# Gaussian elimination split between VectorE and GpSimd: the last eight rows of 128 small systems

## The chip, the cores and the metric

The kernel runs on one core of one Trainium2 chip, as one program of some 90,000 instructions. The metric is the time of one execution on the device in microseconds (us). Before the change the median of three runs is 5004.54 us (5003.34 to 5005.09).

## The reference

Twelve residual blocks act on x, 128 batch entries of 32 tokens with 128 channels. The change touches L0's attention, a kernel attention that solves a linear system for each batch entry and head. Its core, for each of the 128 x 16 pairs of entry and head (8 channels a head):

```python
landmarks = K[:, :, landmark_idx, :]                  # 64 indices into the 32 tokens
Phi_Q = jnp.exp(-C_Q / temperature)                   # C_Q, C_K: squared distances to the landmarks
Phi_K = jnp.exp(-C_K / temperature)
W_kernel = jnp.exp(-W_sq / temperature) + REG * jnp.eye(NUM_LANDMARKS)
Y = jnp.linalg.solve(W_kernel, jnp.einsum('bhnk,bhnd->bhkd', Phi_K, V))
out_unnorm = jnp.einsum('bhnk,bhkd->bhnd', Phi_Q, Y)  # divided by the same with V of ones
```

Since the 64 landmarks are drawn from 32 tokens, the kernel solves a system of 32 rows with 9 right-hand sides (8 value columns and one of ones), with the square roots of each token's count as a diagonal scaling.

The output projection of this is added to x. Before it comes a cross-attention of each entry to 257 context rows with 16 heads; after it comes a feed-forward layer with 8 experts of which each token takes two.

## The kernel before

**Stages.** `L0_xattn` (lines 372 to 476) loops over the 128 batch entries, n = 0 to 127, in eight groups g of 16. For each entry it computes scores on TensorE (S, line 544), takes their maxima on VectorE (L546, L547), exponentials on ScalarE (L548, L558), transposes (L566, L569), multiplies with the context (L583, L584); for each tile of four entries it computes queries (L527) and the output (L597). The last VectorE instruction of an entry is L555 (it writes TL). Evacuations of queries (L528) and of OT (L585) are ScalarE's. Then `L0_ffn` (lines 857 to 911) routes tokens to experts, and the rest of L1 to L3 follows.

**Side work.** L0's attention for a group runs beside the cross-attention of later groups, in generators that yield after each piece:

- `L0_attn_kernels(g)` (613 to 685), in the queue `kq`: phi_k and phi_q. Its masks (M, L249), weights (PW, L671 and L672) and blocked values (Vb, L690) run on GpSimd, except in the last group, where they run on VectorE.
- `L0_attn_solve(g)` (693 to 739), in `sq`: the elimination. Once a group's kernels are written, its solve is appended.
- `L0_attn_out(g)` (741 to 773), in `oq`: four output tiles (Yb, ko, O, kot, kw), appended when the solve ends.

`side_steps` (318) is called after every entry with `side_steps(3, 8)`: three pieces of `kq`, then pieces of `sq` until their yielded costs, in us, sum to 8, then one of `oq`. The yielded number is the planner's own guess of VectorE time. In `L0_ffn` the budgets are 3.0, 4.0 and 6.5. A scheduler then sets the final order of each engine's instructions; TensorE's order in the cross-attention is also fixed by manual dependences (`follow`, `queue`).

**The solve.** A has 128 partitions (16 entries x 8 pairs of heads), and on each the two systems side by side: `A[p, i, h, j]`, 32 rows i, 2 heads h, 41 columns j (32 and 9 right-hand sides). For pivot k: the pivot is clamped and inverted (L712, L713), the scaled row is written to `row` (L716, two buffers), and the rows below are updated in blocks of eight (`RB`): a product into `elt` (L722), then a subtraction in A (L724). In the end ScalarE copies the scaled row back into A (L726). Line 729 and 731 are the back substitution. All of it but the copy is VectorE's. The block of rows 24 to 31 has m x 2 x n = 8 x 2 x 17 = 272 elements a partition for pivots 0 to 23.

Other places that the change touches: `dispatch` makes one-hot tiles SL (L845, three buffers) for 16 small matmuls in each of four calls; `L0_ffn_back` gathers expert outputs into G (six buffers) by GpSimd's indirect DMA, 16 in each of four calls, and adds them to x (L1026).

Of the kernel before, what the change touches and what calls it, by code (L numbers as in the profile page):

```python
# [9 lines left out]
FP = mybir.dt.float32  # L10
# [3 lines left out]
ALU = mybir.AluOpType  # L14
# [4 lines left out]
B, T, C = 128, 32, 128  # L19
NG = 8  # L20
# [148 lines left out]
class Kern:  # L169
# [523 lines left out]
    def L0_attn_solve(self, g):  # L693


        nc, sv = self.nc, self.sv
        HC, R, RB = 2, HD + 1, 8
        N = T + R
        A = sv.tile([128, T, HC, N], FP, tag="A", bufs=2)
        bs = slice(16 * g, 16 * g + 16)  # L700
        wv = self.wd.rearrange("(b n) (g h q) -> g h b n q", n=T, g=8, h=HC)
        zv = self.zd.rearrange("b n (g h e) -> g h b n e", g=8, h=HC)
        for hg in range(8):
            r = slice(16 * hg, 16 * hg + 16)
            for h in range(HC):
                nc.sync.dma_start(A[r, :, h, 0:T], wv[hg, h, bs])
            for h in range(HC):
                (nc.scalar if g == NG - 1 else nc.sync).dma_start(A[r, :, h, T:N], zv[hg, h, bs])
        yield 1.0
        for k in range(T):  # L710
            p = sv.tile([128, HC], FP, tag="p", bufs=2)
            nc.vector.tensor_scalar(p, A[:, k, :, k], 1e-6, None, ALU.max)  # L712
            nc.vector.reciprocal(p, p)  # L713
            n = N - 1 - k
            row = sv.tile([128, HC, N], FP, tag="row", bufs=2)
            nc.vector.tensor_tensor(row[:, :, k + 1:N], A[:, k, :, k + 1:N], p.unsqueeze(2).to_broadcast([128, HC, n]), ALU.mult)  # L716
            yield 0.3 + 0.00107 * HC * n
            for i0 in range((k + 1) // RB * RB, T, RB):
                i0, i1 = max(i0, k + 1), i0 + RB
                m, n = i1 - i0, N - i0  # L720
                t = sv.tile([128, RB * HC * N], FP, tag="t", name="elt")[:, :m * HC * n].rearrange("p (i h j) -> p i h j", i=m, h=HC)
                nc.vector.tensor_tensor(t, A[:, k, :, i0:i1].rearrange("p h i -> p i h").unsqueeze(3).to_broadcast([128, m, HC, n]),  # L722
                                        row[:, :, i0:N].unsqueeze(1).to_broadcast([128, m, HC, n]), ALU.mult)
                nc.vector.tensor_tensor(A[:, i0:i1, :, i0:N], A[:, i0:i1, :, i0:N], t, ALU.subtract)  # L724
                yield 0.12 + 0.00214 * m * HC * n
            nc.scalar.copy(A[:, k, :, k + 1:N], row[:, :, k + 1:N])  # L726
        for k in range(T - 1, 0, -1):
            t = sv.tile([128, RB * HC * N], FP, tag="t", name="elt")[:, :k * HC * R].rearrange("p (i h j) -> p i h j", i=k, h=HC)
            nc.vector.tensor_tensor(t, A[:, 0:k, :, k:k + 1].to_broadcast([128, k, HC, R]),
                                    A[:, k, :, T:N].unsqueeze(1).to_broadcast([128, k, HC, R]), ALU.mult)  # L730
            nc.vector.tensor_tensor(A[:, 0:k, :, T:N], A[:, 0:k, :, T:N], t, ALU.subtract)
            yield 0.12 + 0.00214 * k * HC * R
        Yt = sv.tile([128, RB * HC * N], FP, tag="t", name="Yt")[:, :T * HC * R].rearrange("p (i h j) -> p i h j", i=T, h=HC)
        nc.scalar.copy(Yt, A[:, :, :, T:N])
        yv = self.yd.rearrange("b n (g f) -> g b n f", g=8)
        for hg in range(8):
            nc.sync.dma_start(yv[hg, bs], Yt[16 * hg:16 * hg + 16].rearrange("p i h j -> p i (h j)"))
        self.oq.append(chain([1] * (3 if g < NG - 2 else 0), self.L0_attn_out(g)))
        yield 0.1
# [37 lines left out]
    def dispatch(self, pool, psum, tag, I8, n, k, E, NB):  # L777

        nc = self.nc
# [25 lines left out]
        t = pool.tile([128, E, n], FP, tag="dt")  # L805
# [35 lines left out]
        yield 1  # L841
        ps = psum.tile([128, NB], FP, tag=tag, name="pinv")
        for i in range(n * k):
            SL = pool.tile([128, 128], FP, tag="dSL", bufs=3)
            nc.vector.tensor_scalar(SL, self.j128, qf[:, i, 0:1], None, ALU.is_equal)  # L845
            nc.tensor.matmul(ps, lhsT=SL, rhs=BK[:, i, :], start=i == 0, stop=i == n * k - 1)
            if i % 4 == 3 and i < n * k - 1:
                yield 1
# [170 lines left out]
    def L0_ffn_back(self, m, c, slot, rows, inv, E2, fs):  # L1019
        nc = self.nc  # L1020
        for i in range(8):
            x = self.X[c[i // 4]][:, i % 4, :]
            for j in range(2):
                G = fs.tile([128, 128], FP, tag="G", bufs=6)
                self.gather(G, self.ysd[m], slot[:, i, j:j + 1])
                nc.vector.scalar_tensor_tensor(x, G, E2[:, i, j:j + 1], x, ALU.mult, ALU.add)  # L1026

# [59 lines left out]
    def depool(self, dp, dps, tag):  # L1087
# [32 lines left out]
        for g in range(NG):  # L1120
# [17 lines left out]
            nc.scalar.activation(m, m, AF.Exp, scale=-DT)  # L1138
            G = dp.tile([128, 4, 4, T], FP, tag="G")
            nc.vector.scalar_tensor_tensor(G.rearrange("p i b t -> p (i b t)"), PB, self.pm, m, ALU.is_ge, ALU.mult)  # L1140
            nc.gpsimd.tensor_tensor(G, G, bm, ALU.mult)
            ps = dps.tile([128, 4, 128], FP, tag=tag, name="pdp")
            for i in range(4):
                nc.tensor.matmul(ps[:, i, :], lhsT=G[:, i, :, :], rhs=Uc[:, i, :], start=True, stop=True)
            Dg = dp.tile([128, 4, 128], FP, tag="Dg")
# [789 lines left out]
```

## Time and profile before

| | |
|---|---|
| runs before, median | 5004.54 us (5003.34 to 5005.09) |
| the profiled execution's own time | 5007.62 us |
| its span, first to last instruction | 5005.9 us |
| mean granted TensorE clock | 0.889 |
| busy: TensorE, VectorE, ScalarE, GpSimd | 85%, 68%, 47%, 26% |
| L722 and L724, VectorE | 608 each, 290.0 and 291.2 us |
| L729 and L731, VectorE | 248 each, 126.6 and 126.5 us |
| L0's cross-attention | until about 2108 us |
| solves, first pivot row to end of the copy of Y | from 449.8 us to 2423.1 us |

Engines are PE (TensorE's matmul), PEld (its weight load), DVE (VectorE), ACT (ScalarE), POOL (GpSimd), SP (SyncE). A row of the groups reads: line, engine, operation, tile written <- tiles read, shape, xcount | busy us, mean ns of one | idle time of the engine just before, and what ended it. A row of the windows gives each engine's busy time in a stretch. The timeline gives start in us, length, engine, line, operation.

### The profile page before, as it was taken

What the parts mean: (1) busy time and instruction counts of PE and PEld (TensorE: products, weight loads), DVE (VectorE), ACT (ScalarE), POOL (GpSimd) and SP (SyncE); (2) the same over time, 40 slices, a digit from 0 to 9 for tenths busy, and PEclk for the clock granted to TensorE, in tenths of its full rate; (3) what the DMA queues carried; (4) which work ended last, traced back from release to release, by engine and by line L of the source; (5) the groups of instructions that cost most, each with busy time, mean ns of one, the idle gap of its engine ahead of it and who ended that gap; (6) DMA issues with size and microseconds to landing.
All of it is one profiled execution on the core that took longest, in us unless ns stands there. A gap on an engine that the chain in (4) does not pass through costs nothing. (4 is left out here: it accounts for less than half of the span.)

```text
span 5005.9 us, 90275 instructions
## 1 busy us (share of the span) xinstructions
PE 4248.2 (85%) x33802; PEld 3111.7 (62%) x33802; DVE 3387.4 (68%) x10311; ACT 2347.2 (47%) x6637; POOL 1295.6 (26%) x1309
## 2 busy tenths in 40 slices
PE   7999999999898999875377798898898886879788
PEld 5777676767676776665365565666566653546455
DVE  5336758494948576777655478888898775777444
ACT  4555445454444444432233354545554554763333
POOL 1020211111110202035143513332332332322443
PEclk8999899999999998967677898999999987989677
DMA  4223131314141222255132410111011101000100
GB/s 139 61 60 57 39 66 42 66 39 72 38 72 35 56 53 56 49 121 144 37 107 86 138 35 23 31 29 28 27 29 32 37 20 46 1 1 16 32 14 10
DMA packets 388968, 255.95 MB, mean 51 GB/s; under 512 B 184545, under 2 KB 356961, under 8 KB 388017
## 3 DMA queue, kind: packets, MB, share of 16 engines
q1 hardware_dynamic: 361842, 191.22, 16.1%
q0 software_dynamic: 18240, 58.66, 4.0%
q8 instruction: 266, 4.36, 0.4%
q10 hardware_dynamic: 8448, 0.30, 0.2%
q14 instruction: 172, 1.41, 0.1%
HBM read 211.02 MB, written 39.08 MB: 50 GB/s over the span
## 5 line engine op out<-in xcount | busy, mean ns | idle before, releaser
L218 POOL TENSOR_TENSOR rs<-ve,w_const 128x4 f32<-128x4 f32 (+1 forms) x192 | 189.9, 990 | 1552.1 <-DVE ve L216 1278.4
L544 PE MATMUL S<-cT,q 128*128 128x257 f32 x2048 | 545.5, 407 | 18.5 <-ACT E L548 17.8
L544 PEld LDWEIGHTS S<-cT,q 128*128 128x128 f32 x2048 | 391.0, 201 | 145.7 <-issue 54.6
L546 DVE TENSOR_REDUCE nm<-S 128x1 f32<-128x257 f32 x512 | 214.8, 420 | 335.9 <-PE S L544 334.6
L1389 PE MATMUL S<-cT,QM 128*128 128x289 f32 x1024 | 326.4, 435 | 78.5 <-ACT E L1391 70.5
L548 ACT ACTIVATE E<-S,nm 128x257 f32<-128x257 f32 x512 | 242.3, 474 | 299.8 <-DVE nm L547 298.8
L1391 ACT ACTIVATE E<-S,nm 128x289 f32<-128x289 f32 x512 | 253.4, 499 | 194.8 <-DVE nm L1390 190.9
L722 DVE TENSOR_TENSOR elt<-A,row 128x400 f32<-128x400 f32 (+22 forms) x608 | 290.0, 477 | 6.4
L724 DVE TENSOR_TENSOR A<-A,elt 128x400 f32<-128x400 f32 (+22 forms) x608 | 291.2, 479 | 4.2
L527 PE MATMUL pq<-xT,WQK 128*128 128x128 f32 x2048 | 268.0, 290 | 14.1 <-ACT q L528 14.1
L1389 PEld LDWEIGHTS S<-cT,QM 128*128 128x128 f32 x1024 | 177.5, 198 | 161.8 <-ACT E L1391 72.3
L583 PE MATMUL po<-TA,cN 128*128 128x512 f32 x512 | 271.1, 612 | 4.7 <-DVE xn L224 3.9
L527 PEld LDWEIGHTS pq<-xT,WQK 128*128 128x128 f32 x2048 | 252.5, 200 | 24.7 <-ACT q L528 17.6
L584 PE MATMUL po<-TB,cN 128*128 128x512 f32 x512 | 265.5, 600 | 0.0
L558 ACT ACTIVATE E<-E,sm 128x256 f32<-128x256 f32 x512 | 220.2, 498 | 79.8 <-DVE sm L554 74.9
L241 POOL TENSOR_TENSOR QM<-QT,w_const 128x512 f32<-128x512 f32 x128 | 142.6, 1119 | 434.0 <-PE S L1389 410.7
L1390 DVE TENSOR_REDUCE nm<-S 128x1 f32<-128x289 f32 x512 | 219.8, 449 | 31.1 <-PE S L1389 28.3
L1400 PE MATMUL pt<-w_const,E 128*96 128x128 f32 (+1 forms) x1536 | 234.9, 290 | 0.0
L597 PE MATMUL pout<-WVO,OT 128*128 128x128 f32 x2048 | 234.2, 276 | 0.3 <-ACT OT L585 0.3
L597 PEld LDWEIGHTS pout<-WVO,OT 128*128 128x128 f32 x2048 | 231.7, 192 | 0.9 <-ACT OT L585 0.5
L1400 PEld LDWEIGHTS pt<-w_const,E 128*96 128x96 f32 (+1 forms) x1536 | 181.5, 145 | 61.6 <-issue 37.3
L1721 ACT ACTIVATE E<-S,nm 128x128 f32<-128x128 f32 x512 | 179.9, 397 | 64.6 <-DVE nm L1718 64.6
(526 smaller groups left out, 10357.3 us busy)
## 6 DMA issues: line engine op xcount, KB each, us to landing
cT<-ctxT SPq DMA_DIRECT2D x128, 257.0 KB
cN<-ctx SPq DMA_DIRECT2D x128, 256.0 KB
cT<-ctxT SPq DMA_DIRECT2D x32, 514.0 KB
phik<-PW SPq DMA_DIRECT2D x32, 256.0 KB
phiq<-P SPq DMA_DIRECT2D x32, 256.0 KB
A<-phik SPq DMA_DIRECT2D x128, 64.0 KB
PQ<-phiq SPq DMA_DIRECT2D x32, 256.0 KB
cN<-ctx SPq DMA_DIRECT2D x32, 194.0 KB
```

The source lines that it names most:

```text
L527: self.follow(st, nc.tensor.matmul(ps[:, k, :, :], lhsT=WQK[:, 4 * j + k, cb * 128:(cb + 1) * 128], rhs=t["x"], start=True, stop=True))
L544: self.follow(st, nc.tensor.matmul(S, lhsT=t["QP"][j][:, cb, b, :, :], rhs=t["cT"][b][:, cb, :], start=cb == 0, stop=cb == 1))
L548: nc.scalar.activation(E[:, j, 0:LK], S, AF.Exp, bias=m, accum_out=sm[:, j:j + 1])
L558: nc.scalar.activation(E[:, j, 0:256], E[:, j, 0:256], AF.Copy, scale=sm[:, j:j + 1])
L583: self.follow(st, nc.tensor.matmul(po, lhsT=cN[:, 0, c], rhs=TA, start=True, stop=False), nc.tensor.matmul(po, lhsT=cN[:, 1, c], rhs=TB, s ...
L584: nc.tensor.matmul(po, lhsT=cN[:, 1, c], rhs=TB, start=False, stop=True))
L597: self.follow(st, nc.tensor.matmul(po[:, 0, :], lhsT=OT[:, cb, h, :, :], rhs=WVO[:, cb, h, :], start=h == 0 and cb == 0, stop=False))
L722: nc.vector.tensor_tensor(t, A[:, k, :, i0:i1].rearrange("p h i -> p i h").unsqueeze(3).to_broadcast([128, m, HC, n]), row[:, :, i0:N].uns ...
L724: nc.vector.tensor_tensor(A[:, i0:i1, :, i0:N], A[:, i0:i1, :, i0:N], t, ALU.subtract)
L1389: self.follow(st, nc.tensor.matmul(S, lhsT=t["QM"][:, 0, 4 * j:4 * j + 4, :], rhs=t["cT"][:, b, :], start=True, stop=True))
L1391: nc.scalar.activation(E[:, j, :], S, AF.Exp, bias=nm[:, j:j + 1], accum_out=sm[:, j, b:b + 1])
L1400: self.follow(st, nc.tensor.transpose(pt[0:n, j * 128:(j + 1) * 128], E[:, j, k0:k1], self.ident))
```

## The change

In the solves of groups 0 to 6, the product and the subtraction of the last block (rows 24 to 31, while it is whole, that is for pivots 0 to 23) are GpSimd's, with a buffer of their own (`eltp`), and count 0.01 in the planner's sum. The scaled row has three buffers. To make room, SL has two buffers and G three. The last group's solve stays on VectorE.

```diff
-            row = sv.tile([128, HC, N], FP, tag="row", bufs=2)
+            row = sv.tile([128, HC, N], FP, tag="row", bufs=3)
...
-                nc.vector.tensor_tensor(t, A[:, k, :, i0:i1].rearrange("p h i -> p i h").unsqueeze(3).to_broadcast([128, m, HC, n]),
-                                        row[:, :, i0:N].unsqueeze(1).to_broadcast([128, m, HC, n]), ALU.mult)
-                nc.vector.tensor_tensor(A[:, i0:i1, :, i0:N], A[:, i0:i1, :, i0:N], t, ALU.subtract)
-                yield 0.12 + 0.00214 * m * HC * n
+                eng = nc.vector
+                if g < NG - 1 and i0 == T - RB:
+                    eng = nc.gpsimd
+                    t = sv.tile([128, RB * HC * (RB + R)], FP, tag="tp", name="eltp").rearrange("p (i h j) -> p i h j", i=m, h=HC)
+                eng.tensor_tensor(t, A[:, k, :, i0:i1].rearrange("p h i -> p i h").unsqueeze(3).to_broadcast([128, m, HC, n]),
+                                  row[:, :, i0:N].unsqueeze(1).to_broadcast([128, m, HC, n]), ALU.mult)
+                eng.tensor_tensor(A[:, i0:i1, :, i0:N], A[:, i0:i1, :, i0:N], t, ALU.subtract)
+                yield 0.12 + 0.00214 * m * HC * n if eng is nc.vector else 0.01
...
-            SL = pool.tile([128, 128], FP, tag="dSL", bufs=3)
+            SL = pool.tile([128, 128], FP, tag="dSL", bufs=2)
...
-                G = fs.tile([128, 128], FP, tag="G", bufs=6)
+                G = fs.tile([128, 128], FP, tag="G", bufs=3)
```

## The prediction

> **What bounds the kernel now.** The page gives busy shares first.
>
> ```profile
> PE 4248.2 (85%) x33802; PEld 3111.7 (62%) x33802; DVE 3387.4 (68%) x10311; ACT 2347.2 (47%) x6637; POOL 1295.6 (26%) x1309
> ```
>
> TensorE leads, but these shares average over stages. The groups say what the change touches:
>
> ```profile
> L722 DVE TENSOR_TENSOR elt<-A,row 128x400 f32<-128x400 f32 (+22 forms) x608 | 290.0, 477 | 6.4
> L724 DVE TENSOR_TENSOR A<-A,elt 128x400 f32<-128x400 f32 (+22 forms) x608 | 291.2, 479 | 4.2
> ```
>
> VectorE never waits before these 581 us of elimination. By shape, the part that moves (columns as on the page):
>
> ```profile
> L724 DVE TENSOR_TENSOR A<-A,elt 128x272 f32<-128x272 f32 x192 | 84.0, 437 | 0.2
> L722 DVE TENSOR_TENSOR elt<-A,row 128x272 f32<-128x272 f32 x192 | 83.2, 433 | 1.5
> ```
>
> The stage decides. I cut one group of 16 batch entries (1507.8 to 1776.5 us, 268.7 us) at the ends of the L555 row, which closes each entry; call the stretches A, B, C and so on. Columns: length, then busy PE, PEld, DVE, ACT, POOL, granted clock, DMA share, GB/s.
>
> ```profile
> 1507.80:1540.30 32.50, 27.08 (x187) 21.74 (x186) 24.89 (x79) 12.23 (x33) 1.27 (x1) 0.84 0.09 26
> 1540.30:1550.80 10.50, 10.26 (x64) 8.00 (x63) 8.82 (x33) 6.02 (x19) 0.00 (x0) 1.00 0.18 52
> 1550.80:1568.80 18.00, 16.50 (x83) 11.63 (x82) 17.84 (x61) 5.99 (x20) 2.38 (x4) 1.00 0.12 32
> 1568.80:1576.90 8.10, 8.07 (x53) 6.48 (x52) 7.97 (x31) 6.61 (x21) 0.00 (x0) 1.00 0.23 65
> 1576.90:1593.20 16.30, 14.54 (x76) 11.02 (x76) 15.99 (x60) 9.62 (x28) 0.00 (x0) 1.00 0.12 34
> 1593.20:1601.50 8.30, 7.96 (x47) 6.03 (x46) 8.16 (x34) 5.79 (x20) 0.00 (x0) 1.00 0.23 64
> 1601.50:1626.10 24.60, 19.64 (x168) 14.24 (x169) 21.81 (x88) 10.97 (x34) 7.68 (x9) 1.00 0.08 24
> 1626.10:1645.70 19.60, 17.44 (x228) 11.91 (x218) 18.89 (x42) 9.84 (x27) 6.67 (x5) 0.87 0.16 46
> 1645.70:1669.30 23.60, 23.44 (x246) 18.95 (x242) 22.20 (x58) 11.65 (x27) 5.13 (x4) 0.82 0.14 48
> 1669.30:1684.80 15.50, 14.31 (x95) 9.79 (x96) 6.49 (x26) 7.65 (x20) 1.04 (x1) 0.78 0.44 68
> ```
>
> A solve runs in A to J. In C to F VectorE is 98% busy: it sets the pace there, with TensorE only some 5% behind. In I and J TensorE sets it. So a microsecond of VectorE work is worth about a microsecond in C to F, less in A, B and G, and little in I and J. After 2108 us, outside this stage, the last solve (which the change leaves on VectorE) ends at 2423 us, with TensorE waiting 76 us for what follows it.
>
> **What is removed.** 24 pivots (0 to 23) of seven solves: 168 pairs of 272 elements. Busy time is 0.87 us a pair, but VectorE instructions overlap their neighbours (an L722 of 272 elements starts at 1539.00 and the next instruction at 1539.35), so a pair frees 0.70 us: 16.8 us a solve, 118 us in all.
>
> **Where it is freed.** The planner still places 8 us of side work an entry, and counts a GpSimd pair as 0.01. I compared both built orders between the L555 rows, each two-input instruction of N elements taken as 0.07 us + 1.04 ns x N (0.35 us at 272). Change of solve work: A -3.9, B +2.2, C -2.6, D -1.1, E -2.0, F -1.7, G +4.5, H -2.5, I -9.0, J -0.8; sum -16.9. More than half the relief lands in I and J, where TensorE is the limit.
>
> **What is added.** 336 GpSimd instructions. None of this shape is in the trace; the nearest rows (GpSimd by shape, 430 to 2110 us):
>
> ```profile
> L690 POOL TENSOR_TENSOR Yb<-Y,bmD 128x576 f32<-128x576 f32 x24 | 28.7, 1196 | 148.3 <-PE ko L756 131.9 <-PE pq L527 8.1 <-DMA Y<-yd 5.0
> ...
> L605 POOL TENSOR_TENSOR xn<-xn,w_L_xln 128x128 f32<-128x128 f32 x25 | 12.2, 487 | 2.0
> ```
>
> A line between 0.49 us at 128 and 1.20 at 576 gives 0.72 us at 272; with L671 (1327 ns at 512) as the upper end, 0.80. I take 0.72: 1.44 us a pair, 34.6 us a solve. GpSimd has room (20% busy in this stage), except in E, where eight pairs fall: 11.5 of 16.3 us.
>
> **What they cost VectorE.** Here a rule speaks against the change, and the timeline has a row for it (start, length):
>
> ```profile
> 1643.40 0.60 DVE L729 TENSOR_TENSOR elt<-A 128x432 f32<-128x432 f32 x1
> ...
> 1644.07 1.04 POOL L249 TENSOR_TENSOR M<-QT,hq 128x512 f32<-128x512 f32 x1 [9.82 <-PE kc L658]
> 1644.18 1.40 DVE L731 TENSOR_TENSOR A<-A,elt 128x432 f32<-128x432 f32 x1
> ```
>
> The same 432 elements take 0.60 us alone and 1.40 when started 0.11 us into a GpSimd instruction: VectorE stands until GpSimd is done. The Trainium skill ("SBUF — State Buffer", section "Who interferes with whom") states it: a VectorE instruction with two SBUF inputs and a GpSimd instruction that reads SBUF exclude each other for a whole instruction. Every elt, A and row instruction has two. By the rule at its worst a pair costs VectorE its full 1.44 us, twice what it frees: +17.8 us a solve. By the rows it is less, since VectorE also runs one-input work (the maxima from PSUM, copies, reciprocals) behind which GpSimd hides. I took the 43 GpSimd tensor instructions that lie amid solve work (at least three solve instructions starting within 2.5 us on each side): 39.2 us of their own, for which VectorE instructions started during them ran 16.4 us over their usual length, 0.42 us per us. These 43 fall at chance places; the new ones follow a row instruction, when VectorE's next is a two-input one. I take 0.5, with 0.15 and 1.0 as ends: 0.72 us a pair, all of what it frees. By stretch (4, 3, 3, 3, 8, 3 pairs in A to F): +2.9, +2.2, +2.2, +2.2, +5.8, +2.2.
>
> **New waits.** The row instruction of pivot k waits for GpSimd's (or ScalarE's) use of row k-3; ScalarE's copy L726 waits for GpSimd's multiply where it waited for VectorE's (236 us in 140 waits already, mostly harmless), with exponentials and the evacuation of queries queued behind it; softmax maxima queue behind the row. With three rows and GpSimd keeping up I price these at nothing (cover gone: the difference of paces, some 1 us a pivot in E and F). Pivot 24 reads what GpSimd wrote last: one pair, +1.4 us in F.
>
> **What moves along.** In the order before, two of four output tiles of the previous group sit in A, where VectorE stands 4.8 us:
>
> ```profile
> L758 DVE TENSOR_SCALAR nm<-ko 32x32 f32<-32x32 f32 x4 | 0.7, 170 | 4.8 <-PE ko L756 4.8
> ```
>
> The solve ends sooner in the new order, so they sit in J and K. A then looks like the first group's A (27.1 us, no such tiles, 11 block updates as now): 27.1 + 0.6 for larger blocks + 2.9 = 30.6, or -1.9. J and K take one each, at some 2.5 us: the stretch after K is 12.7 us with such a tile and 10.6 in the first group, which has none, and A's two cost 5.4.
>
> **Sum.** A -1.9; B +2.2+2.2-1.7 (idle) = +2.7; C -0.4; D +1.1; E +3.8; F -1.7+2.2+1.4 = +1.9; G +4.5 less half its 2.8 us idle = +3.1; H -1.5 (down to its TensorE time and a little); I -2.5 (half the 5 us that a clock of 0.82 costs); J +1.5 (a tile, less VectorE work and some of its clock loss); K +2.5. Together +10.3 us a group. Six groups +62; the seventh solve's A to D +1.5; its other 11 pairs, behind the stage, -7.7+7.9+1.4 = +1.6. The two buffers cut: G is issued every 1.25 us and lands in 2.7, so three in flight nearly sustain it; SL is made in fours behind matmuls. From 0 to +8, I take +3. Total +68 on the execution's 5007.6 (span 5005.9): 5076; the median run is 3.1 shorter: 5073.
>
> **Rivals.** (1) Serial: nearly every pair meets two-input work and ScalarE's queue stands behind it. Fraction 1.0 adds 17.3 us a solve, +121: 5194. For it: E's eight pairs in a VectorE already full. Against: the measured 0.42. (2) Faster: GpSimd runs mostly behind one-input work and idle time, fraction 0.15: 12.1 us less a solve, 85 in all: 4988. It decides where the fraction falls below about 0.22 (68 us over 7 x 34.6 under 0.5). For it: in C to F about a third of VectorE's time is one-input work. Against: the row above. (3) Nothing visible, at that crossing. That the work isn't moved is excluded by the built order, which has all 336 on GpSimd.
>
> **Chances.** Main case 0.62, serial 0.15, faster 0.16, no change 0.07. The range 4985 to 5140 leaves out the far half of the faster case (fractions under 0.15, the clock held up better than assumed) and most of the serial one. A measurement of this kernel can tell about 0.2% from no change: faster 0.16, within 0.2% 0.07, slower 0.77.
>
> **What would show it.** Right: L722 and L724 on VectorE lose 168 each but their remaining shapes grow longer, by 0.5 us per us of GpSimd's pairs; C to F lengthen, E most; A shortens; GpSimd pairs of 1.4 to 1.6 us. Wrong: remaining shapes at their old lengths (rival 2), or E above 25 us with TensorE waiting for ScalarE's queries (rival 1), or pairs above 2 us.

## The result and the profile after

The changed kernel takes 5135.02 us (median of three runs, 5130.35 to 5137.06), against 5004.54 before: the ratio is 1.0259, with a 95% interval of 1.0236 to 1.0283. The profiled execution took 5130.35 us, its span is 5128.6. L0's cross-attention ends at 2221.2 us instead of 2108.5, so 112.7 of the span's 122.7 us arise in that stage.

The shares, and the four groups that were two. The GpSimd pair has a row of its own now:

```profile
PE 4249.5 (83%) x33802; PEld 3092.6 (60%) x33802; DVE 3400.3 (66%) x9975; ACT 2352.2 (46%) x6637; POOL 1575.6 (31%) x1645
```

```profile
L728 DVE TENSOR_TENSOR A<-A,elt 128x400 f32<-128x400 f32 (+28 forms) x440 | 249.4, 567 | 4.4
L726 DVE TENSOR_TENSOR elt<-A,row 128x400 f32<-128x400 f32 (+28 forms) x440 | 239.8, 545 | 6.3 <-DVE row L716 0.2
L726 POOL TENSOR_TENSOR eltp<-A,row 128x272 f32<-128x272 f32 x168 | 136.0, 810 | 405.1 <-DVE row L716 361.8 <-DVE nm L547 23.9 <-DVE sm L553 19.4
L728 POOL TENSOR_TENSOR A<-A,eltp 128x272 f32<-128x272 f32 x168 | 143.0, 851 | 13.1
L547 DVE TENSOR_TENSOR nm<-nm,nsn 128x1 f32<-128x1 f32 x512 | 122.0, 239 | 8.3
L712 DVE TENSOR_SCALAR p<-A 128x2 f32<-128x2 f32 x256 | 60.7, 237 | 13.7 <-POOL A L728 10.2 <-POOL on L796 0.7
```

VectorE has 336 instructions fewer and is busy for 13 us more. (Lines from the elimination on are four higher than before: L722 is L726, L724 is L728, ScalarE's copy is L730.) The same group of 16 entries, A to J, in the columns of the table shown of before:

```profile
1586.20:1616.70 30.50, 23.07 (x112) 17.55 (x111) 22.18 (x61) 11.91 (x32) 7.73 (x8) 0.84 0.09 27
1616.70:1628.50 11.80, 11.29 (x70) 8.71 (x70) 11.34 (x34) 6.40 (x20) 4.19 (x5) 0.99 0.17 46
1628.50:1646.00 17.50, 14.92 (x73) 10.60 (x72) 16.48 (x50) 5.55 (x19) 8.64 (x11) 1.00 0.11 33
1646.00:1656.10 10.10, 8.37 (x53) 6.40 (x51) 9.96 (x31) 7.17 (x22) 4.53 (x6) 1.00 0.17 52
1656.10:1679.60 23.50, 15.34 (x73) 11.47 (x72) 21.34 (x63) 9.65 (x30) 12.95 (x16) 0.90 0.08 23
1679.60:1692.60 13.00, 9.37 (x40) 6.26 (x40) 9.51 (x38) 6.19 (x22) 4.32 (x6) 0.89 0.15 42
1692.60:1721.30 28.70, 24.13 (x185) 17.39 (x183) 25.35 (x74) 11.59 (x32) 9.82 (x9) 0.95 0.08 20
1721.30:1736.60 15.30, 13.29 (x166) 9.09 (x170) 15.02 (x40) 6.73 (x18) 5.63 (x4) 0.88 0.19 58
1736.60:1761.60 25.00, 24.68 (x253) 20.27 (x240) 13.65 (x41) 13.65 (x31) 4.78 (x4) 0.80 0.19 34
1761.60:1776.50 14.90, 13.96 (x182) 9.82 (x181) 7.28 (x26) 7.12 (x21) 3.39 (x3) 1.00 0.43 123
```

E, where eight pairs fall, went from 16.3 to 23.5 us with almost the same work on TensorE (73 matmuls, 76 before). H and I have much less VectorE work than before (I 13.65 us busy instead of 22.20). H is shorter (15.3 us instead of 19.6), but I is not.

What happens in E shows in two microseconds of its timeline (start, length, engine, line, operation, and in brackets the idle time before with its releaser):

```profile
1671.59 0.20 DVE L716 TENSOR_TENSOR row<-A,p 128x44 f32<-128x44 f32 x1
1671.83 0.39 DVE L726 TENSOR_TENSOR elt<-A,row 128x220 f32<-128x220 f32 x1
1671.94 0.81 POOL L726 TENSOR_TENSOR eltp<-A,row 128x272 f32<-128x272 f32 x1 [0.68 <-DVE row L716]
1672.25 0.74 DVE L728 TENSOR_TENSOR A<-A,elt 128x220 f32<-128x220 f32 x1
1672.78 0.23 ACT L730 COPY A<-row 128x44 f32<-128x44 f32 x1 [2.18 <-POOL eltp L726]
1672.82 0.79 POOL L728 TENSOR_TENSOR A<-A,eltp 128x272 f32<-128x272 f32 x1
1672.91 0.58 ACT L585 COPY OT<-po 128x512 f32<-128x512 f32 x1
1673.02 0.61 DVE L712 TENSOR_SCALAR p<-A 128x2 f32<-128x2 f32 x1
1673.67 0.17 DVE L713 RECIPROCAL p<-p 128x2 f32<-128x2 f32 x1
```

VectorE's L726 and L728 both have 220 elements. The first takes 0.39 us. The second starts at 1672.25, inside GpSimd's multiply, and takes 0.74: it ends at 1672.99, 0.24 after GpSimd's end at 1672.75. Then the clamp of the pivot, two elements, starts 0.20 us into GpSimd's subtraction (1672.82 to 1673.61) and ends 0.02 after it: 0.61 us instead of 0.16. Each half of the pair makes one VectorE instruction longer, by 0.35 and by 0.45 us.

### The profile page after: what moved, and what is told of

Same layout as the page of the kernel before. It is cut to its first block, busy times and chain, and to the rows that moved or that the text cites. A ratio compares the mean times of both kernels' runs of the same rounds, so it can differ in the third digit from the quotient of the medians.

```text
span 5128.6 us, 90613 instructions
## 1 busy us (share of the span) xinstructions
PE 4249.5 (83%) x33802; PEld 3092.6 (60%) x33802; DVE 3400.3 (66%) x9975; ACT 2352.2 (46%) x6637; POOL 1575.6 (31%) x1645
## 5 line engine op out<-in xcount | busy, mean ns | idle before, releaser
L546 DVE TENSOR_REDUCE nm<-S 128x1 f32<-128x257 f32 x512 | 214.5, 419 | 374.6 <-PE S L544 373.8
L548 ACT ACTIVATE E<-S,nm 128x257 f32<-128x257 f32 x512 | 242.9, 475 | 382.8 <-DVE nm L547 382.5
L726 POOL TENSOR_TENSOR eltp<-A,row 128x272 f32<-128x272 f32 x168 | 136.0, 810 | 405.1 <-DVE row L716 361.8
L728 DVE TENSOR_TENSOR A<-A,elt 128x400 f32<-128x400 f32 (+28 forms) x440 | 249.4, 567 | 4.4
L726 DVE TENSOR_TENSOR elt<-A,row 128x400 f32<-128x400 f32 (+28 forms) x440 | 239.8, 545 | 6.3 <-DVE row L716 0.2
L585 ACT COPY OT<-po 128x512 f32<-128x512 f32 x256 | 148.9, 583 | 157.0 <-PE po L584 155.2
```

Of the source, the lines that this page charges most:

```text
L548: nc.scalar.activation(E[:, j, 0:LK], S, AF.Exp, bias=m, accum_out=sm[:, j:j + 1])
L726: eng.tensor_tensor(t, A[:, k, :, i0:i1].rearrange("p h i -> p i h").unsqueeze(3).to_broadcast([128, m, HC, n]), row[:, :, i0:N].unsqueeze ...
L728: eng.tensor_tensor(A[:, i0:i1, :, i0:N], A[:, i0:i1, :, i0:N], t, ALU.subtract)
```

## The experiments

The theory: the loss is made by GpSimd's pairs while they run, since VectorE stands behind them. The rivals: the planner's order (pairs counted as 0.01, so the solve is packed into earlier entries and two output tiles move), the cut buffers, and the new waits (for the row, for A, for ScalarE's copy). Each kernel ran beside the kernel before; the median of the latter was 5049.1, 5049.8 and 4994.2 us in the three sets of runs, so the ratios are compared, and one per mille is 5 us. "A group" below is the mean length of 16 entries (A to P) over five groups in a row, the one shown being the last of them: 267.5 us before, 286.1 after.

**e1_buffers.** The kernel before with the three buffer counts alone:

```diff
-            row = sv.tile([128, HC, N], FP, tag="row", bufs=2)
+            row = sv.tile([128, HC, N], FP, tag="row", bufs=3)
...
-            SL = pool.tile([128, 128], FP, tag="dSL", bufs=3)
+            SL = pool.tile([128, 128], FP, tag="dSL", bufs=2)
...
-                G = fs.tile([128, 128], FP, tag="G", bufs=6)
+                G = fs.tile([128, 128], FP, tag="G", bufs=3)
```

> The kernel before with only the buffers changed (row 3, SL 2, G 3), all elimination on VectorE. Theory (the loss is made by GpSimd's pairs running against VectorE's two-input instructions): the buffers cost next to nothing, 5004 to 5012 us. Rival (the cut buffers cost what the stage does not show, some 10 us behind it): 5012 to 5020 us.

Measured: 1.0013 (1.0003 to 1.0023), a group 267.5 us. The buffers cost some 6 us, and none of it shows in the five groups. The interval is too wide to part the two expectations.

**e2_left_out.** The kernel after without the pair (rows 24 to 31 are not updated for pivots 0 to 23):

```diff
+                if eng is nc.gpsimd:
+                    yield 0.01
+                    continue
                 eng.tensor_tensor(t, A[:, k, :, i0:i1]...
```

> The kernel after with GpSimd's pair left out and done by nobody: rows 24 to 31 are not updated for pivots 0 to 23, in the planner still 0.01 each. Theory (GpSimd's pairs make the loss while they run): the loss goes and the relief of VectorE shows, 4960 to 5005 us. Rival (the planner's order, which packs the solve into earlier entries and moves two output tiles, makes the loss): most of it stays, 5080 us or more.

Measured: 0.9993 (0.9981 to 1.0005), a group 266.3 us. The loss is gone, and next to no gain comes of it: 118 us of VectorE's work, done by nobody, are worth some 10 us against e1, which has the same buffers (1.0013 less 0.9993, give or take some 8 us), and nothing that can be told from zero against the kernel before. The built order is nearly the changed kernel's: the stretches A to G hold 4, 3, 4, 2, 8, 7 and 4 pivots here, and 4, 3, 4, 2, 8, 6 and 5 there. The same 440 updates, 512 maxima and 256 clamps as in the groups of after, in this kernel's lines:

```profile
L731 DVE TENSOR_TENSOR A<-A,elt 128x400 f32<-128x400 f32 (+28 forms) x440 | 211.9, 482 | 4.2
L729 DVE TENSOR_TENSOR elt<-A,row 128x400 f32<-128x400 f32 (+28 forms) x440 | 211.4, 481 | 6.4
L547 DVE TENSOR_TENSOR nm<-nm,nsn 128x1 f32<-128x1 f32 x512 | 100.7, 197 | 8.3
L712 DVE TENSOR_SCALAR p<-A 128x2 f32<-128x2 f32 x256 | 42.6, 169 | 2.8
```

After minus this: 37.5 + 28.4 + 21.3 + 18.1 = 105.3 us by which VectorE took longer in these four groups. With L555 (22.1 to 29.4 us) and L551 (20.5 to 23.7) it is 115.8 us: 0.69 us for each of 168 pairs, 0.42 us for each of GpSimd's 279.0.

**e3_order_only.** The kernel after with the pair on VectorE, still counted as 0.01. The planner's order is then the changed kernel's; the scheduler still puts some steps elsewhere (E holds 6 pivots instead of 8).

```diff
+                own = eng is nc.gpsimd
+                eng = nc.vector
...
-                yield 0.12 + 0.00214 * m * HC * n if eng is nc.vector else 0.01
+                yield 0.01 if own else 0.12 + 0.00214 * m * HC * n
```

> The kernel after with the pair given back to VectorE, still counted as 0.01 by the planner: the order of the changed kernel without any work on GpSimd. Theory: each pair costs VectorE 0.70 us in the crowded entries instead of the standing behind GpSimd; 4 us a group more than before, 5015 to 5060 us, clearly under the changed kernel. Rival (the order makes the loss): 5120 to 5150 us, as the changed kernel. If moving the pair did relieve VectorE: above the changed kernel.

Measured: 1.0115 (1.0093 to 1.0137), a group 276.6 us. This order has a cost of its own, 9.1 us a group where VectorE does the pairs, of which 4 were expected (B +4.1, G +3.5, A +3.2, K +2.6, H -4.2), and the changed kernel is still 9.5 a group worse.

**e4_no_read.** The pair replaced by memsets of the same two tiles, so that GpSimd writes and does not read (rows 24 to 31 are set to 1 instead of updated):

```diff
+                if eng is nc.gpsimd:
+                    eng.memset(t, 1.0)
+                    eng.memset(A[:, i0:i1, :, i0:N], 1.0)
+                    yield 0.01
+                    continue
```

> The kernel after with both GpSimd instructions of a pair replaced by memsets of the same two tiles (the update of rows 24 to 31 is left out, they are set to 1): GpSimd still runs and writes 336 times in the same places, but reads no SBUF, and neither the pivot rows nor ScalarE's copies wait for it. Theory (GpSimd's reads of SBUF hold VectorE): within 15 us of the kernel with the pair left out, 4965 to 5020 us. Rival (any GpSimd instruction in flight holds VectorE, or the wait of pivot 24 does it): 5050 us or more.

Measured: 1.0000 (0.9987 to 1.0014), a group 266.1 us, as with the pair left out. This is no test of writing, since the memsets did not run in the pairs' places: nothing of VectorE's paces them. The 168 of eltp were done 70.4 us into the execution, before any solve, and those of A ran in bursts of 24 once a solve's A had been loaded. Only 16 of VectorE's updates started inside a memset; these kept their lengths within 0.01 us. So e4 repeats e2, and that it is GpSimd's reading that counts is not shown by it.

**e5_old_count and e6_left_old_count.** The planner counts the pair at its old 0.70; once with the pair on GpSimd, once with it left out (rows 24 to 31 as in e2). The built order comes out unlike that of before, though: E holds 8 to 11 pivots in both, and 5 in the kernel before.

```diff
-                yield 0.12 + 0.00214 * m * HC * n if eng is nc.vector else 0.01
+                yield 0.12 + 0.00214 * m * HC * n
```

> The kernel after with the planner counting GpSimd's pair at its old cost (0.70) in place of 0.01: the same work on GpSimd, in the order of before. The runs so far: in the changed order the pairs cost nothing when left out, 62 us on VectorE, 134 us on GpSimd; order and buffers alone made 58 us. Theory (GpSimd's pairs cost some 20 us a group in whatever order, the changed order 9 on top): ratio to before 1.010 to 1.022, A to F longer than before, G and K not. Rival (the pairs are dear only because the changed order puts eight of them in E): 1.000 to 1.008.

> The kernel after with GpSimd's pair left out, as before, but counted at its old cost: the order of before without the work (rows 24 to 31 are not updated for pivots 0 to 23). It gives what VectorE's relief is worth at most. Theory (VectorE sets the pace in C to F, TensorE stands some 5% behind): 3 to 7 us a group shorter, ratio 0.990 to 0.996. Rival (the relief is worth its 16.8 us a solve): 0.977.

Measured: 1.0196 (1.0177 to 1.0215) and 0.9985 (0.9975 to 0.9996), a group 280.1 and 264.4 us. In e5 E grew more than in the changed kernel (25.8 us, with ten pairs in it in the group of the table above) and G (26.3) and K (22.0) less. e6 missed what was expected (0.990 to 0.996): the relief is worth less. Taken together, six kernels with the same buffers:

| a group, us (ratio to before) | pair left out | on VectorE | on GpSimd |
|---|---|---|---|
| counted 0.70 | 264.4 (0.9985) | 267.5 (1.0013) | 280.1 (1.0196) |
| counted 0.01 | 266.3 (0.9993) | 276.6 (1.0115) | 286.1 (1.0259) |

On GpSimd the 24 pairs cost 15.7 or 19.8 us a group over not doing them, 0.65 to 0.83 us each. On VectorE they cost 3.1 or 10.3 us, 0.13 or 0.43 each, of the 0.70 that was reckoned for them. The VectorE figures are the looser ones, since the number of pivots in a stretch changes with the pair (E: 5 in the kernel before, 8 to 11 in e6; 6 in e3, 8 in e2).

**e7_four_rows and e8_late_copy.** Four buffers for the row, then also ScalarE's copy of row k issued after the updates of pivot k + 1:

```diff
-            row = sv.tile([128, HC, N], FP, tag="row", bufs=3)
+            row = sv.tile([128, HC, N], FP, tag="row", bufs=4)
...
-            nc.scalar.copy(A[:, k, :, k + 1:N], row[:, :, k + 1:N])
+            if late:
+                nc.scalar.copy(*late.pop())
+            late.append((A[:, k, :, k + 1:N], row[:, :, k + 1:N]))
+        nc.scalar.copy(*late.pop())
```

> The kernel after with four buffers for the scaled row in place of three. Theory (the loss is the standing of VectorE behind GpSimd's instructions and the reverse, not the wait for a row): as the changed kernel, ratio to before 1.022 to 1.029. Rival (row k waits for GpSimd's and ScalarE's use of row k-3): 1.005 to 1.018, and E shorter than 23 us.

> The kernel with four rows, in which ScalarE's copy of a scaled row into A is issued one pivot later, so that it no longer waits for the GpSimd multiply of its own pivot, with the exponentials queued behind it. Theory: the copy's wait is a small part; within 0.4% of the kernel with four rows. Rival (TensorE's 98 us of waiting for exponentials come from ScalarE standing at the copy): 0.8% to 1.5% under it.

Measured: 1.0244 (1.0225 to 1.0264) and 1.0257 (1.0235 to 1.0278); a group 285.3 and 285.9 us, E 23.5 in both. The wait for a row does not make the loss. e8 is inconclusive: ScalarE still stands at the copies behind GpSimd's multiply (52.7 us in the cross-attention, 50.9 in after), so the later issue did not free it. The next kernel settles the copy.

**e9_private.** The pair on private data (the row times itself, minus the row, in eltp; rows 24 to 31 are not updated): same size and reads, and A is not touched by GpSimd.

```diff
+                    rb = row[:, :, i0:N].unsqueeze(1).to_broadcast([128, m, HC, n])
+                    eng.tensor_tensor(t, row[:, :, i0:i1].rearrange("p h i -> p i h").unsqueeze(3).to_broadcast([128, m, HC, n]), rb, ALU.mult)
+                    eng.tensor_tensor(t, t, rb, ALU.subtract)
```

> The kernel after with GpSimd's pair working on private data: it multiplies the scaled row with itself into eltp and subtracts the row from that (the update of rows 24 to 31 is left out). The same reads of SBUF, length and pacing by the row, but A is not written: pivot 24 waits for nothing of GpSimd's, ScalarE's copy waits for no multiply. Theory (VectorE stands behind GpSimd's instructions, 0.73 us a pair in the trace of after): nearly all of the changed kernel's loss, ratio to before 1.018 to 1.027. Rival (the waits through A make it): 1.000 to 1.010.

Measured: 1.0231 (1.0205 to 1.0257), a group 283.2 us, E 23.2. Against e2 the pair costs 16.9 us a group, of the changed kernel's 19.8, though nobody waits for its result and no copy for its multiply. That is 0.70 us for each of 24 pairs, as much as the lengthening counted under e2. The waits through A are worth the rest at most, 2.9 us a group. ScalarE's copies no longer stand behind GpSimd here, and TensorE's waits for exponentials and queries in the cross-attention (us in total, times, longest), 96.5 and 30.1 us in after, are nearly as long:

```profile
PE S L544 <- ACT E L548: 91.0, 46, 5.0
PE pq L527 <- ACT q L528: 26.5, 19, 2.0
```

**e10_twice.** GpSimd's multiply issued twice:

```diff
+                if eng is nc.gpsimd:
+                    eng.tensor_tensor(t, A[:, k, :, i0:i1]..., row[:, :, i0:N]..., ALU.mult)
                 eng.tensor_tensor(t, A[:, k, :, i0:i1]..., row[:, :, i0:N]..., ALU.mult)
```

> The kernel after with GpSimd's multiply issued twice, the second over the first: 168 more GpSimd instructions of some 0.8 us, nothing else. Theory: 0.4 to 0.5 us of VectorE for each us of GpSimd, in stretches that VectorE paces, 50 to 75 us more than the changed kernel: ratio to before 1.035 to 1.042. Rival (GpSimd's length does not matter, only that it is waited for): within 0.4% of the changed kernel.

Measured: 1.0364 (1.0339 to 1.0388), a group 293.1 us, E 26.1. Its three GpSimd groups take 411.4 us, 132.4 more than after's two. The time grew by 0.0105 of 5004.5, 53 us: 0.40 us for each added us on GpSimd.

**e11_budget7 and e12_budget6.** With VectorE's relief worth so little where it is, I tried placing the solve differently in the kernel before, with less side work an entry:

```diff
-                        self.side_steps(3, 8)
+                        self.side_steps(3, 7)
```

> The kernel before with the planner's side work in the cross-attention cut from 8 to 7 us an entry, all elimination on VectorE. Theory (the solve's place in the group decides, since A to F are paced by VectorE and L to P leave it idle): C to F shorter, the later stretches longer, ratio 0.993 to 1.000. Rival (the solve that ends later runs into the heavy TensorE stretches): 1.000 to 1.008.

> The same with 6 us an entry. Theory: 0.988 to 1.000. Rival: 1.002 to 1.015.

Measured: 0.9993 (0.9984 to 1.0003) and 1.0010 (1.0001 to 1.0018); a group 266.3 and 267.2 us. What some stretches gain (in e11 J 15.0 to 12.5, H 19.6 to 16.3) A and G give back; C to F, expected shorter, are not (C 18.0 to 19.3). e12 lies between its two expectations. None of these versions beats the kernel before by more than 0.2%.

## Why the prediction came out so

The sign held, and so did the mechanism of the loss: the pairs lengthen VectorE's instructions. The gain set against it did not come. The time lies in the range, but 5 us under its upper end (5073 forecast, 5135 measured, 5140 the end): the loss was forecast at 68.5 us and measured at 130.5. Of the 62 us between them some 50 lie in the six groups: 18.6 us each instead of 10.3. e2 splits the change of each stretch in two, what order and relief do without the pairs and what the pairs do (measured: means of five groups).

| us | A | B | C | D | E | F | G | H | I | J | K | sum |
|---|---|---|---|---|---|---|---|---|---|---|---|---|
| relief and order, forecast | -4.8 | +0.5 | -2.6 | -1.1 | -2.0 | -1.7 | +3.1 | -1.5 | -2.5 | +1.5 | +2.5 | -8.6 |
| measured, e2 minus before | -3.1 | 0.0 | -2.2 | -0.7 | +0.7 | +0.6 | +4.3 | -3.9 | +0.8 | -0.2 | +2.6 | -1.1 |
| pairs on GpSimd, forecast | +2.9 | +2.2 | +2.2 | +2.2 | +5.8 | +3.6 | 0 | 0 | 0 | 0 | 0 | +18.9 |
| measured, after minus e2 | +2.8 | +2.7 | +1.7 | +2.5 | +6.7 | +3.8 | -0.4 | -0.2 | +0.1 | +0.2 | 0.0 | +19.9 |

- **What the pairs cost VectorE: right.** Forecast 0.72 us a pair, half of GpSimd's time, from 43 chance meetings at 0.42; measured 0.69, at 0.42 us per us of longer pairs (1.66 us instead of 1.44, above the 1.60 that the forecast's upper reading gives). That the product fits so well is luck: the share was taken too high and the pair too short, and the two errors cancel. The sample is loose, too: over the 100 GpSimd tensor instructions of the kernel before that have three solve instructions of any kind starting within 2.5 us before and after their start, it would have given 0.27. The rule of the Trainium skill that stood behind it ("SBUF — State Buffer", "Who interferes with whom") agrees with the rows above, where an instruction that starts inside GpSimd's ends after it; that GpSimd's reads alone do it, as the section says, no run here shows. The worst case, the pair's full length, did not occur: maxima from PSUM beside a pair kept their length (44 started inside one).
- **Where it is freed: the step that failed.** The forecast freed 0.70 us a pair and gave -8.6 a group for relief and moved work; it was -1.1. In C and D the forecast was near (-2.9 measured, -3.7 forecast). Of the 7.5 us between forecast and measurement, E and F make 5.0, I 3.3, A 1.7, G 1.2; H and J, better than forecast, give 4.1 back.
- **E and F:** the 0.70 was a distance from start to start, taken where independent work stood on both sides. VectorE in E of the kernel before:

```profile
1587.11 0.16 DVE L712 TENSOR_SCALAR p<-A 128x2 f32<-128x2 f32 x1
1587.23 0.57 DVE L724 TENSOR_TENSOR A<-A,elt 128x400 f32<-128x400 f32 x1
1587.72 0.16 DVE L713 RECIPROCAL p<-p 128x2 f32<-128x2 f32 x1
1587.84 0.44 DVE L722 TENSOR_TENSOR elt<-A,row 128x272 f32<-128x272 f32 x1
1588.20 0.20 DVE L716 TENSOR_TENSOR row<-A,p 128x50 f32<-128x50 f32 x1
1588.32 0.44 DVE L724 TENSOR_TENSOR A<-A,elt 128x272 f32<-128x272 f32 x1
```

And in E of the kernel with the pair left out, with the rows of its E and F (columns as above) ahead:

```profile
1568.00:1584.80 16.80, 14.82 (x83) 11.60 (x82) 15.60 (x63) 10.23 (x31) 0.00 (x0) 1.00 0.10 31
1584.80:1593.60 8.80, 7.92 (x41) 5.50 (x40) 8.21 (x42) 6.26 (x23) 0.00 (x0) 1.00 0.23 63
```

```profile
1577.11 0.17 DVE L712 TENSOR_SCALAR p<-A 128x2 f32<-128x2 f32 x1
1577.31 0.17 DVE L713 RECIPROCAL p<-p 128x2 f32<-128x2 f32 x1
1577.58 0.21 DVE L716 TENSOR_TENSOR row<-A,p 128x46 f32<-128x46 f32 x1
1577.82 0.45 DVE L729 TENSOR_TENSOR elt<-A,row 128x276 f32<-128x276 f32 x1
1578.31 0.45 DVE L731 TENSOR_TENSOR A<-A,elt 128x276 f32<-128x276 f32 x1
1578.79 0.17 DVE L712 TENSOR_SCALAR p<-A 128x2 f32<-128x2 f32 x1
```

Before, the steps of the next pivot lie between the updates of other blocks, the pair among them, and each starts 0.04 to 0.08 us before its neighbour ends. Without the pair, each step needs the one before it and starts 0.03 to 0.10 us after its end: p, reciprocal and row alone take 0.71 us from the first's start to the next's. In the mean of five groups, VectorE's durations in E sum to 19.6 us in 16.1 before, and to 17.5 us in 16.8 without the pairs. The work fell by 2.1 us, as forecast, and the stretch grew by 0.7: it became a chain. The pair had filled that chain's gaps, and the new order makes the chain longer: E holds 8 pivots without the pairs and 5 before, F 7 and 3. How much of the miss is the lost filling and how much the added pivots, the runs do not separate. The forecast summed the work of two-input instructions in the built order and gave the steps from pivot to pivot no price.

- **I:** forecast -2.5, by half of what a clock of 0.82 costs (5 us in the forecast; its own row, 23.44 us of TensorE at 0.82, gives 4.2). VectorE's work in I fell and the granted clock stayed (0.82 before, 0.79 in e2, 0.82 after): that relief was taken where TensorE alone decides. In J the clock went from 0.77 to 1.00, with the output tiles and the earlier end of the solve, which is where H and J gained; what the runs don't separate is how much of that is the clock's.
- **A, G, J, K:** the moved tiles came as read from the built order; K was met. A's miss is one of reading: the forecast gave every group the A of one, which was 32.5 us. The first of the five has no earlier group's tiles in its A (27.1 us before, 27.8 in e2), so it had none to lose. In the other four A fell by 4.1 us on average, and by 4.7 in the group that the forecast was read from.
- **New waits, priced at nothing: right for the row.** The row instruction waited 0.3 us in the whole execution, and four rows changed nothing. The waits through A are at most the 2.9 us a group between e9 and after; 1.4 (pivot 24) was forecast, and the clamp stood idle for GpSimd's subtraction for 10.2 us in seven solves, 1.5 each.
- **Buffers:** +3 forecast (0 to 8), some 6 measured.
- **Behind the stage:** +1.6 and +3 forecast; the profiled executions differ by 10.1 us there. With e1's 6 the rest, 4, is not resolved: kernels without any pair differ there by 8 (e1 2946.1, e6 2954.1).
- **Rival 1, serial:** excluded by 0.42 us of VectorE per us of GpSimd (0.50 of the kernel's time, 19.9 us a group for 39.9), and E stayed under 25 us. TensorE's wait for exponentials did grow, from 16.7 to 96.5 us in the stage. Half of that, 50.4 us, is there with the pair left out, and ScalarE itself waits longer for VectorE's maxima (L548 behind L547, in the whole execution: 382.5 us, 298.8 before). So the maxima come late; and with the copies freed from GpSimd in e9 TensorE still waits 91.0 us, so ScalarE's queue is not what holds it.
- **Rival 2, faster:** excluded more firmly than forecast. It was to decide below a fraction of 0.22 and give 4988 at 0.15. With a fraction of zero, that is e2, the time is 0.9993 of before (0.9981 to 1.0005): even pairs that held nobody up would have ended within 0.2% of before.

## What to carry to other kernels

Before moving work off an engine, run the kernel with that work simply left out: here 118 us of VectorE's time were worth some 0.2 to 0.3% (e2 and e6 against e1), so the move could hardly win. Price freed time from the chain that remains, not from start to start: independent instructions between dependent ones can be cheap (0.13 and 0.43 us a pair here, instead of 0.70), and taking them away leaves their gaps. The work given to GpSimd here cost a busy VectorE some 0.4 us per us, and counting it as nearly nothing in the planner cost another 6 us a group (286.1 against 280.1).

## What the runs showed of the hardware

- The clamp of the pivot, a TENSOR_SCALAR with one SBUF input of 128x2, also stood behind GpSimd (0.61 us instead of 0.16; its 256 took 60.7 us in after, 42.6 with the pair left out). I had counted only instructions with two inputs. The 512 maxima read from PSUM (L546, 214.5 us in after, 215.2 with the pair left out) did not lengthen, though 44 of them started inside a pair.
- GpSimd stands behind VectorE as well: the multiply of 272 elements took 0.67 us at its quickest in E and 0.99 where VectorE's updates of 400 met it, so a pair's price on GpSimd depends on what VectorE does.
- The 16 updates of VectorE that started inside a GpSimd memset in e4 kept their length within 0.01 us. They are few, and no run puts GpSimd writes alone beside the elimination.
- In E, where VectorE held TensorE up, the granted clock fell too: 1.00 before and in e2, 0.86 after and 0.81 in e10 (means of five groups). TensorE took 15.34 us for 73 matmuls there, 14.54 for 76 before. D, which grew from 7.5 us in e2 to 10.1 after, stayed at 1.00, so what sets the clock is left open.
